# Half of the x transposes moved from TensorE to VectorE, and the first loads in another order

## The chip, the cores and the metric

The kernel runs on one core of a Trainium2 chip. A core has five engines that run at the same time, each with its own queue of instructions: TensorE (PE: matrix products, and transposes as products with an identity matrix; its weight loads are listed as PEld), VectorE (DVE), ScalarE (ACT), GpSimd (POOL) and SyncE (SP, which here only issues transfers). An engine works through its queue in the order in which the instructions stand there. PE's results go to PSUM, eight banks of 128 partitions x 512 numbers; everything else lies in SBUF, 128 partitions wide. Transfers between DRAM and SBUF run on 16 DMA engines; SP, ACT and POOL issue them.

The metric is the device time of one execution in microseconds (us), less is better. The kernel before takes 1168.65 us, the median of three runs (1167.21 to 1170.46).

## The reference

All numbers are float32. Four sequences of 512 tokens with 512 features each go through two layers (weight names without their prefix):

```python
# layer 0, V = 512, hidden size 4 V = 2048
q, k, v = x @ Wq, x @ Wk, x @ Wv
attn = softmax(einsum('btd,bTd->btT', q, k) * V ** -0.5)
attn_out = einsum('btT,bTd->btd', attn, v) @ Wp + bp
cms_out = gelu(attn_out @ cW1 + cb1) @ cW2 + cb2 + one_hot(target_codes)[:, None, :]
modifier = gelu(concat([attn_out, cms_out]) @ mW1 + mb1) @ mW2 + mb2
x = clip(x + cms_out + modifier, 0, 1)
# layer 1: an adapter chosen per sequence from three (stream)
h = gelu(x @ W_down[stream] + b_down[stream]) @ W_up[stream] + b_up[stream]
out = layernorm(x + h) * ln_w[stream] + ln_b[stream]
```

## The kernel before

**Products.** Every large product is split by a scheme with seven half-sized products in place of eight, and most of them twice. The price is sums of blocks, ahead of the products (operands) and behind them (results). The function `seven` (L622) runs the products in a given order; 1, 5 and 6 each open a PSUM bank, and 2, 7, 4 and 3 add to a bank that is there. Between them DVE makes sums on those banks: after 5 `c15 = ps + c1`, after 6 `y = x + c15`, after 7 `v = x + c15`, after 4 `x = x + c1`. Product 7 adds to the bank x and so waits until y has been made from it; product 4 waits in the same way until v has been made; product 3 adds to y. `pair_product` (L663) handles two sequences at once; one product in it is four matmuls of 128 x 512 (L668), some 3.43 us. `small_product` works on one 512 x 512 matrix (L734).

**The first stage.** Wq and Wk are turned on PE (L899) and folded into one matrix Wq Wk^T, likewise Wv and Wp into Wv Wp, so that scores are x (Wq Wk^T) x^T and the output is (softmax x) (Wv Wp). Sequences come in two pairs. For a pair the code makes x^T of both sequences (`first_operand`, `both_operands`), the product u with the folded Wq Wk^T (`pair_product` with `beside_u`, which makes the sums of u beside it), the two score products with softmax, softmax times x, and the product with the folded Wv Wp.

**How x is turned.** `begin_transposed` (L500) takes four PSUM banks and does 16 PE transposes of 128 x 128 (L505); its `end` copies each bank to SBUF on ACT and makes the block sums on DVE straight from PSUM. x1 and x2 are turned at the start. x3 and x4 are turned during the first pair's product with Wv Wp, after product 6 and after product 4 (`then`, L1011). That product and the next pair's first one then share the eight banks with the transposes.

**How Wv is turned.** `begin_turned` (L518) uses DVE's own transpose, which turns blocks of 32 x 32: `load_blocks` (L151) lays Wv in SBUF in such a way that turning the blocks alone gives Wv^T, with a fixed order of the features; Wp's rows are loaded in the same order. Four DVE transposes of 128 x 512 (L522) write four banks. They read every fourth element of a partition (`p (t c d) -> p d t c`). Transposes and sums are hung behind product 6 of the first pair's u product.

**Loads and places.** SP issues Wq in four quarters, x1, x2, Wv's four pieces, Wp. ACT issues Wk, later the stores of x^T (`xT_kept`) and of the attention output. POOL issues the first unit of cW1 and the rows of x3 and x4, then forms sums of weights for later stages (`expansion`), which it stores to DRAM; it also makes the block sums of x (`left_sums`) and of Wp (`right_sums`, L767). Large tiles are used several times: `slot[2]` and `slot[3]` hold Wv and Wp, `slot[4]` and `slot[5]` cW1's unit, `slot[6]` and `slot[7]` x3 and x4 by rows.

**Order.** A scheduler lays the instructions into each engine's queue; `tc.keep_in_program_order` pins single ones, and `steps` releases portions of POOL's expansion work behind a given instruction. A transfer issued by SP or ACT uses one of eight semaphores in turn, and waits for the transfer that last used it.

**Later.** The hidden layers (L1179, L1269, L1337, L1437 are their products) read weights through SP; `with_input` (L1717) reads `xT_kept` back and adds it to the result on POOL (L1719, L1722).

## Time and profile before

| what | us |
|---|---|
| median of three runs | 1168.65 |
| the profiled execution | 1168.84 |
| its span, first to last instruction | 1166.9 |
| PE busy | 1156.4 |
| DVE, POOL, ACT busy | 888.9, 589.2, 293.5 |
| first stage (attention, both pairs) | 0 to about 242 |
| first and second hidden layers, adapters | about 242 to the end |

The granted clock of PE is 0.999 of full speed. The profile's groups give the line of the code, engine, operation, and the tiles as out<-in with buffer numbers left out, followed by partitions x elements and the count; in the timeline start and length come first, and in brackets the idle time before the instruction and what ended it. A float32 matmul is recorded as two PE instructions, so one of 128 x 512 takes 0.857 us in two records. Busy times of single PE records overlap, since matmuls are pipelined; starts are the better measure. The chain of work that ended last gives start, length and work.

### The profile page before, as it was taken

The numbers are of one execution on the slowest core, as the hardware profiler recorded it, in microseconds if no ns is written. First come the engines' busy times: TensorE is split into PE (matmuls) and PEld (weight loads), VectorE is DVE, ScalarE is ACT, GpSimd is POOL, SyncE is SP. The second block draws the span as 40 slices with busy tenths as digits, with TensorE's granted clock in tenths as the row PEclk, the third lists the DMA queues.
The fourth block names the chain that finished last, engine by engine and source line by source line (L and its number), as shares of the span: only waits on it lengthen the run. The fifth ranks groups of instructions, "written<-read, shape, count | busy, mean of one in ns | idle before, by whom it ended". The sixth has DMA issues, their size and how long they took to land.

```text
span 1166.9 us, 13700 instructions
## 1 busy us (share of the span) xinstructions
PE 1156.4 (99%) x4973; PEld 925.0 (79%) x4973; DVE 888.9 (76%) x1219; ACT 293.5 (25%) x535; POOL 589.2 (50%) x652
## 2 busy tenths in 40 slices
PE   9999999999999999999999999999999999999997
PEld 7588558656468888888888887778888888888875
DVE  6855555467699967899699956689994588689956
ACT  4244316236520000012310037271000003230014
POOL 4889999988998057872200626972000001242101
PEclk9999999999999999999999999999999999999999
DMA  9762784997776588896847562146745455594701
GB/s 300 277 201 85 296 319 147 341 375 268 276 256 244 180 276 311 330 327 257 261 154 275 195 215 90 64 146 181 295 136 189 163 218 179 176 309 165 248 6 72
DMA packets 82450, 256.78 MB, mean 220 GB/s; under 512 B 7972, under 2 KB 41040, under 8 KB 67024
## 3 DMA queue, kind: packets, MB, share of 16 engines
q1 hardware_dynamic: 58032, 152.98, 36.8%
q0 software_dynamic: 21968, 93.37, 22.6%
q10 hardware_dynamic: 2384, 9.57, 2.0%
q8 instruction: 39, 0.64, 0.2%
q14 instruction: 27, 0.22, 0.1%
HBM read 186.69 MB, written 66.06 MB: 217 GB/s over the span
## 4 chain that ended last, share of the span: by engine, by line
PE 93%; DVE 4%; DMA 1%; issue 1%; DVEq 0%; SPq 0%
PE i L1437 29%; PE i L1337 24%; PE sum L734 10%; PE sum L1179 9%; PE sum L668 8%; PE c L1269 6%; PE down_ps L1543 2%; PE up_ps L1562 2%; DVE hidden L578 1%; PE tr_ps L505 1%; DMA wslot<-in_L_cond_mW 1%; DVE part L1041 1%; DVE slot L219 1%; PE up_ps L1557 1%; DMA wide<-in_L_cond_Wq 0%
## 5 line engine op out<-in xcount | busy, mean ns | idle before, releaser
L1337 PE MATMUL i<-slot,wslot 128*128 128x256 f32 x1184 | 261.5, 379 | 1.8 <-DVE part L1041 1.7
L1337 PEld LDWEIGHTS i<-slot,wslot 128*128 128x128 f32 x1184 | 224.7, 190 | 33.4 <-issue 1.8
L1437 PE MATMUL i<-slot,wslot 128*128 128x256 f32 x896 | 202.5, 379 | 0.0
L1437 PEld LDWEIGHTS i<-slot,wslot 128*128 128x128 f32 x896 | 170.2, 190 | 23.1
L1048 ACT COPY first<-i 128x256 f32<-128x256 f32 (+1 forms) x56 | 26.8, 479 | 518.7 <-PE i L1437 245.1
L1437 PE MATMUL i<-hidden,wslot 128*128 128x256 f32 x576 | 132.2, 379 | 0.0
L1437 PEld LDWEIGHTS i<-hidden,wslot 128*128 128x128 f32 x576 | 109.4, 190 | 15.7 <-issue 1.0
L1041 DVE TENSOR_TENSOR part<-i,part 128x512 f32<-128x512 f32 (+1 forms) x156 | 90.8, 591 | 36.8 <-PE i L1337 25.5
L1070 ACT ACTIVATE hidden<-hidden,bias 128x512 f32<-128x512 f32 x128 | 83.9, 716 | 79.1 <-DVE hidden L578 69.1
L1719 POOL DMA_DIRECT2D slot<-xT_kept x4 | 2.8, 692 | 152.9 <-PE i L1337 152.9
L1179 PE MATMUL sum<-mod,wslot 128*128 128x256 f32 x288 | 66.6, 379 | 0.0
L1179 PEld LDWEIGHTS sum<-mod,wslot 128*128 128x128 f32 x288 | 54.7, 190 | 7.4
L1041 DVE TENSOR_TENSOR part<-i,first 128x512 f32<-128x512 f32 (+1 forms) x62 | 36.3, 589 | 29.2 <-PE i L1337 17.5
L1722 POOL TENSOR_TENSOR cms<-cms,slot 128x512 f32<-128x512 f32 x16 | 22.4, 1419 | 69.9 <-PE i L1337 41.5
L219 DVE TENSOR_TENSOR slot<-hidden 128x1024 f32<-128x1024 f32 x46 | 57.6, 1252 | 0.0
L219 DVE TENSOR_TENSOR slot<-hidden,slot 128x1024 f32<-128x1024 f32 x46 | 56.7, 1233 | 0.3
L578 DVE TENSOR_TENSOR hidden<-part,hidden 128x2048 f32<-128x2048 f32 x20 | 55.0, 2748 | 0.5
L1269 PE MATMUL c<-slot,wslot 128*128 128x512 f32 x128 | 55.3, 592 | 0.0
L578 DVE TENSOR_TENSOR sum<-sum,wslot 128x512 f32<-128x512 f32 x48 | 33.2, 695 | 29.0 <-PE sum L734 19.2
L734 PE MATMUL sum<-hidden,wslot 128*128 128x256 f32 x232 | 53.2, 379 | 0.0
L1269 PEld LDWEIGHTS c<-slot,wslot 128*128 128x128 f32 x128 | 24.3, 190 | 30.6 <-issue 28.2
L734 PEld LDWEIGHTS sum<-hidden,wslot 128*128 128x128 f32 x232 | 43.8, 190 | 5.8
(339 smaller groups left out, 2123.9 us busy)
## 6 DMA issues: line engine op xcount, KB each, us to landing
wslot<-m_kept SPq DMA_DIRECT2D x48, 1024.0 KB, 6.4
wslot<-m_kept SPq DMA_DIRECT2D x36, 512.0 KB, 5.1
wslot<-c_kept SPq DMA_DIRECT2D x16, 1024.0 KB, 6.7
slot<-in_L_cond_mW POOLq DMA_DIRECT2D x24, 512.0 KB, 6.8
wslot<-in_L_cond_mW SPq DMA_DIRECT2D x24, 512.0 KB, 6.7
wslot<-in_L_cond_cW SPq DMA_DIRECT2D x40, 256.0 KB, 6.3
slot<-in_L_cond_cW POOLq DMA_DIRECT2D x16, 512.0 KB, 7.1
m_kept<-wide POOLq DMA_DIRECT2D x6, 1024.0 KB, 7.0
```

Source lines behind the costliest of these rows:

```text
L219: i = eng.tensor_tensor(out_, one, two, ALU.subtract)
L578: nc.vector.tensor_tensor(dst, a, b, ALU.add)
L668: nc.tensor.matmul(ps, lhsT=lhs[p][:, c, r * P : (r + 1) * P], rhs=rhs[p][:, c, :], start=(first_ and c == 0), stop=(c == 1), skip_group_c ...
L734: nc.tensor.matmul(v[:, j, :], lhsT=lhs[p][:, c, j * P : (j + 1) * P], rhs=rhs[p][:, c, :], start=(first_ and j == 0 and c == 0), stop=(c ...
L1041: nc.vector.tensor_tensor(dst, ps, other, ALU.add)
L1048: nc.scalar.copy(c1, p1)
L1070: nc.scalar.activation(block[:, t, :], block[:, t, :], AF.Gelu, bias=bias_c[:, 8 * half + t : 8 * half + t + 1],)
L1179: nc.tensor.matmul(halves_of(ps)[:, j, :], lhsT=a[g][:, at_[q], j * P : (j + 1) * P], rhs=rhs[q][:, 0, :], start=(first_ and j == 0), stop ...
L1269: nc.tensor.matmul(ps, lhsT=lhs(c, t), rhs=operands[p][:, c, :], start=(c == 0), stop=(c == 1),)
L1337: nc.tensor.matmul(out_ps[:, j, :], lhsT=a[j][q][:, c, :], rhs=now[q][:, c, :], start=(c == 0), stop=(c == 1),)
L1437: nc.tensor.matmul(ps[:, :256], lhsT=a[k // 2][q][:, k % 2, :], rhs=now[q][:, k, :], start=(k == 0), stop=(k == 3),)
L1543: nc.tensor.matmul(ps, lhsT=wd[:, c, n * P : (n + 1) * P], rhs=y[:, c, tokens], start=(c == 0), stop=(c == NV - 1),)
```

## The change

1. x3 and x4 are loaded as blocks by SP (`load_blocks`, four transfers each) into `slot[6]` and `slot[7]` and turned by DVE, as Wv is (`begin_x` chooses). Their rows, which `left_sums` and a later product need, are loaded by SP into the same places after the turning. x1 and x2 stay on PE, but all x^T now hold feature 4p+d in partition p, chunk d; so the PE transposes of x1 and x2 read their weights with a step of four elements, Wq and Wk are loaded with that order of rows, and `xT_kept` is written and read with it.
2. Wv's DVE transposes read 32 neighbouring elements (`p (t d c)`); Wp's rows are loaded to match, in four transfers.
3. SP issues, after x1 and x2, Wp, the first unit of cW1 (formerly POOL's), and Wv last. Wv lies in `slot[6]`, Wp in `slot[7]`, until x3 and x4 take these.
4. Wv's transposes are still hung behind product 6, its copies and sums now behind product 7. Wp's sums on POOL stand ahead of the first expansion steps, which are released behind the last of them.

```diff
-                out=w[:, 2 * r : 2 * r + 2, columns],
-                in_=src[rows, columns].rearrange("(c p) n -> p c n", p=P),
+                out=w[:, chunks, columns],
+                in_=src.rearrange("(p c) n -> p c n", c=4)[:, chunks, columns],
...
-    x_rows = [load_x(b, nc.sync, x_places[b]) for b in range(2)]
-
-    def load_blocks(src, dst, eng):
+    def load_blocks(src, dst, eng, order="p (t c d) -> p d t c"):
...
-        return dst.rearrange("p (t c d) -> p d t c", d=4, c=32)
-
-    wv = load_blocks(Wv, slot[2], nc.sync)
-    wp = slot[3].rearrange("p (c n) -> p c n", c=4)
-    nc.sync.dma_start(out=wp, in_=Wp.rearrange("(p c) n -> p c n", c=4))
+        return dst.rearrange(order, d=4, c=32)
+
+    x_rows = [load_x(b, nc.sync, x_places[b]) for b in range(2)]
+
+    def load_c1(u, eng):
...
+    wp = rows_of(slot[7])
+    for a in range(4):
+        nc.sync.dma_start(
+            out=wp[32 * a : 32 * a + 32],
+            in_=Wp[P * a : P * a + P].rearrange("(c p) n -> p c n", p=32),
+        )
+    load_c1(0, nc.sync)
+    wv = load_blocks(Wv, slot[6], nc.sync, "p (t d c) -> p d t c")
...
-        load_c1(0)
-
-        for b in range(2, B):
-            x_rows.append(load_x(b, nc.gpsimd, x_places[b]))
-        yield from expand_c1(0, lambda: load_c1(1))
+        yield from expand_c1(0, lambda: load_c1(1, nc.gpsimd))
...
-            nc.gpsimd.tensor_tensor(out_, one, two, ALU.subtract)
+            i = nc.gpsimd.tensor_tensor(out_, one, two, ALU.subtract)
+            if out_ is t1:
+                tc.keep_in_program_order(i)
+        behind.append(i)
...
-    xT_kept = [spill.tile([P, 4, 512], F32, name=f"xT_kept{b}") for b in range(B)]
+    xT_kept = [spill.tile([V, T], F32, name=f"xT_kept{b}") for b in range(B)]
...
+    def begin_x(b, dst, finish):
+        if b > 1:
+            return begin_turned(x_blocks[b - 2], dst, finish)
+        return begin_transposed(
+            lambda c: x_rows[b][:, c, :].rearrange("p (n d) -> p d n", d=4), dst, finish
+        )
...
         for k in range(2):
-            nc.scalar.dma_start(out=xT_kept[2 * pair + k], in_=xT[k])
+            nc.scalar.dma_start(
+                out=xT_kept[2 * pair + k].rearrange("(p c) n -> p c n", c=4), in_=xT[k]
+            )
+            if pair:
+                x_rows.append(load_x(2 + k, nc.sync, x_places[2 + k]))
...
+            rhs_wp = right_sums(wp, w_vp)
             steps(expanding, 2)
             s_v = sums_in(slot[2])
-            rhs_wp = right_sums(wp, w_vp)
-            then[6] = [lambda: begin_turned(wv, wv_t, left_from_psum(wv_t, s_v))()]
+            then[6] = [lambda: ends.append(begin_turned(wv, wv_t, left_from_psum(wv_t, s_v)))]
+            then[7] = [lambda: ends[1]()]
...
+            x_blocks = [load_blocks(x[b], flat(x_places[b]), nc.sync) for b in range(2, B)]
...
-            tc.keep_in_program_order(nc.gpsimd.dma_start(out=in_rows[3], in_=xT_kept[2 * pair + s]))
+            tc.keep_in_program_order(nc.gpsimd.dma_start(out=in_rows[3], in_=xT_kept[2 * pair + s].rearrange("(c p) n -> p c n", p=P)))
```

## The prediction

> **What bounds the kernel now.** I read the page's busy shares first, then the list of who made TensorE (PE) wait, then the chain that ended last, and only then the timeline around the places that the change touches.
>
> ```profile
> PE 1156.4 (99%) x4973; PEld 925.0 (79%) x4973; DVE 888.9 (76%) x1219; ACT 293.5 (25%) x535; POOL 589.2 (50%) x652
> ```
>
> ```profile
> PE i L1337 <- DVE part L1041: 1.7, 2, 1.4
> PE idle_ps L204 <- DVE zeros L201: 1.1, 1, 1.1
> PE sum L668 <- DVE sum L578: 0.9, 1, 0.9
> PE tr_ps L899 <- DMA wide<-in_L_cond_Wq: 0.4, 2, 0.2
> ```
>
> PE works through 1156.4 of 1166.9 us, and all its waits sum to 4.1 us. So only two things move the end: PE instructions that are removed or become longer, and waits of PE. The third wait line (0.9 us) lies where Wv is turned. In the chain (start, length, work) the reader is to see the transposes of the four x (L505, 16 each) as ordinary PE work in the row, and Wv's four VectorE (DVE) transposes (L522):
>
> ```profile
> 15.91 1.75 PE tr_ps L505 x16
> ...
> 23.03 1.90 PE tr_ps L505 x16
> 24.92 13.75 PE sum L668 x32
> 39.30 4.12 DVE tr_ps L522 x4
> 46.91 3.70 PE sum L668 x8
> ...
> 127.85 1.75 PE tr_ps L505 x16
> ...
> 134.00 3.44 PE sum L668 x8
> 137.44 1.64 PE tr_ps L505 x15
> 139.08 26.61 PE sum L668 x62
> ```
>
> The timeline at Wv: the transposes hold DVE's queue, eight small sums follow, and only then the two additions for which PE's product 4 waits.
>
> ```profile
> 39.30 4.11 DVE L522 STREAM_TRANSPOSE tr_ps<-slot 128x512 f32<-128x512 f32 x4
> ...
> 46.17 1.28 DVE L578 TENSOR_TENSOR sum<-sum,wslot 128x512 f32<-128x512 f32 x2
> ...
> 46.91 3.70 PE L668 MATMUL sum<-mod,cms 128*128 128x512 f32 x8 [0.88 <-DVE sum L578]
> ```
>
> **The change, part by part.** The sum is made against the profiled execution, 1168.84 us (span 1166.9 and 1.9 around it), 0.2 above the median of 1168.65.
>
> *PE loses the transposes of x3 and x4:* 16 at 127.85 (1.75 us), 15 at 137.44 (1.64) and a single one at 133.72 (0.11): 3.50 us, all in PE's row without a gap.
>
> *DVE gains eight transposes.* Price: the L522 row, 4.11 / 4 = 1.03 us each; they too read with a step of four elements. In the changed program's order they stand between DVE's additions. I follow that queue with the old starts. The sum for product 5 starts at 124.52 and the next can start 0.60 later. First transpose 125.12 to 126.15; addition for product 6 at 126.17, when PE delivers, as before; second transpose 126.77 to 127.80; addition at 127.88; third and fourth 128.48 to 130.54; eight small sums (2.74 in the old row at 130.34) to 133.25; then the addition that product 4 needs, 0.70 long, done at 133.95. PE now starts product 7 at 127.68 (where the transposes began), 3.43 for four matmuls, then three matmuls of product 3 (0.857 each): 133.68. So it waits 0.3 us. Below, the wait could be nothing; above, 1.0, the four transposes' 4.1 less the 3.1 of DVE idle time between 122.73 and 127.88 that they can fill. I take 0.3. For x4 the same walk has three transposes from 134.6 to 137.7, one addition, the fourth transpose to 139.4, and the first t1 that the next product 5 needs at 140.0; PE reaches it at 133.95 + 3.43 + 0.86 + 3.43 = 141.7, and its second chunk's t1 is done at 141.6 where it is wanted at 142.5. About a microsecond is left, so nothing is added. Gain of both: 3.50 - 0.3 = 3.2.
>
> *Wv's transposes read 32 neighbouring elements instead of every fourth.* No row shows a contiguous DVE transpose. Ends: 1.03 as now, or 0.60, the step from one 512-wide DVE instruction to the next (139.41 to 140.01). In the new order two, not eight, of the small sums stand ahead of product 4's addition, but PE also arrives earlier, since only half of product 3 stands ahead of product 4: 41.93 + 1.71 = 43.64 instead of 45.86. At 1.03 the addition ends at 39.30 + 4.11 + 0.68 + 0.70 = 44.8: PE waits 1.15, against 1.05 before and 0.18 of slow starts around it: gain 0.1. At 0.60 it ends at 43.1: no wait, gain 1.2. I take 0.60: source and destination are as in the 512-wide rows, and the step of four is what goes. Gain 1.2.
>
> *x1 and x2 stay on PE, but its weight loads now read every fourth element* (x[:, 4p+d]). All PE rows here read with step one, 1.75 / 16 = 0.109 us each. Low end: 0. High end, if a PE read is paced as the L522 row (1.03 us / 512 = 2.0 ns an element): 128 x 2.0 = 0.257 us, so 32 x 0.148 = 4.7 us, all of it on PE's row. I take 0, since the same instruction on the same engine is the nearest row, and keep 4.7 for the range; it is the largest doubt here.
>
> The Trainium skill (SBUF - State Buffer, section Door 1, its note on cachelines) speaks against this part: lines of 16 bytes, of which an access needs two hits to run at full rate. The 2.0 ns an element of the L522 row against 1.2 for a unit-step instruction fits it, though no run here shows it for PE. By that rule the 32 weight loads would about double, an estimate of 3.5 us, and the sum below would be 0.9 instead of 4.4.
>
> *Queues.* SP takes over four cW1 loads and Wp's, now four, ahead of Wv's four; later eight block loads and two row loads of x. POOL drops six issues (about 0.75 each) and its idle 9.7 us before L209 at 32.24 shrinks. No PE wait is on POOL, so this counts nothing. Hidden too: x3's and x4's blocks are issued when Wv's and Wp's buffers come free (from about 43 and 62) for use at 125 and 134; their rows again after their transposes, at 130.5 and 139.4, for POOL's sums at 157.8 and 191.2 (in_x rows took 9.5 to 17.9 us to land). POOL would queue behind them if late, and PE only at 188.6. SP has nothing else to issue until 205.5. Wq and Wk keep their pieces of 1 KB. The reads of xT_kept in pieces of 2 KB instead of 8 delay POOL's L1722 sums, which end at 579.5 in the first pair; DVE first uses them at 630. ACT's store of x2's transpose waits for a piece of Wp, issued about 20 us earlier: nothing.
>
> *Sum:* 3.2 + 1.2 - 0 = 4.4; 1168.84 - 4.4 = **1164.4 us**.
>
> **The rivals.**
> 1. *The strided weight loads cost.* For: the L522 row. Against: none of its time is PE's. At 1.7 times (1.03 / 0.60) 32 x 0.076 = 2.4 us, at the high end 4.7: 1166.8 to 1169.1, most likely about 1167.8. PE does the same work for x1 and x2 in more time than it saved on half of it.
> 2. *The contiguous transpose stays at 1.03.* 3.2 + 0.1: 1165.5.
> 3. *Slower: Wv lands late.* Its loads are now last, behind Wp and 2.1 MB of cW1, and each waits for an earlier load to land. DVE meets them at 39.3 in front of product 4's addition, and PE waits behind. From x's end (issued at 5.1, 9.5 to land: 14.6 us), Wp, cW1, Wv and the two stores of xT_kept are 6.3 MB; at the mean of 281 GB/s in the first 60 us that is 22.4 us: landed at 37.0. At 246 GB/s, what the DMA engines moved from 14 to 22 us while Wv and Wp came in, 40.2, already on the edge; at the 202 of the slowest 2 us in it, 45.8. It decides from about 39.9 on, and the time passes the old one when Wv lands after 44.3; a landing at 46 to 49 gives 1170.5 to 1173.5. Against: cW1, two x and the stores ran at 396 GB/s from 22 to 40 us; with that for cW1 and the stores (4.2 MB, 10.6 us) and 246 for Wp and Wv (2.1 MB, 8.5 us) Wv lands at 33.7. The same side holds a wait for x's rows or blocks that I have not seen.
>
> **How the numbers follow.** Chances: forecast 0.42 (own range 1163.3 to 1165.6), rival 1 0.31, rival 2 0.12, rival 3 0.15. About 0.3% (3.5 us) is what a measurement of this kernel can tell from no change; faster by more than that means below 1165.1. The forecast lies there for 0.37 of its 0.42, rival 2 for 0.04, rival 1 for 0.01: 0.42. Slower by over 0.3%, above 1172.2, is most of rival 3: 0.13. The rest, 0.45, is within. The range from 1163.2 to 1169.8 leaves out most of rival 3 and the edges of the others.
>
> **What would show it.** In the changed profile: L505's counterpart with two groups of 16 PE transposes fewer, and the two that stay (near 16 and 23 us) at 1.75 us each if step four is free, 3 to 4 us if rival 1 holds; Wv's DVE transposes at about 0.6 us and no PE wait near 44 us, or 1.03 and a wait of 1.1; the eight for x at 1.03 and a PE wait of 0.3 near 133. A DVE transpose released by a DMA near 40 us would show rival 3. After 140 us every PE start should be earlier by one constant; if it is not, a wait I have not named took the place.

## The result, and the profile after

| what | before | after |
|---|---|---|
| median of eight runs | 1168.77 us (1167.21 to 1170.46) | 1174.74 us (1170.64 to 1176.03) |
| the profiled execution | 1168.84 | 1174.30 |
| its span | 1166.9 | 1172.5 |

The ratio after to before is 1.0045 (95% interval 1.0029 to 1.0061): the changed kernel is slower by about half a per cent, where 1164.4 us, 0.4% faster, was forecast. Single executions lie up to 2 us from the median before and up to 4 us after; below, the profiled ones are compared with each other, and the medians decide whether a version is faster.

The page's first view, busy time, share of the span and instructions by engine, of after:

```profile
PE 1156.0 (99%) x4941; PEld 923.4 (79%) x4941; DVE 900.2 (77%) x1227; ACT 294.4 (25%) x535; POOL 596.7 (51%) x646
```

PE has 32 records fewer, as the change says, and is busy 0.4 us less, although the span is 5.6 us longer. So PE must have stood still somewhere; and since 3.5 us of transposes are gone, some of what remains must have become longer. Who made PE wait, in after (in total, times, longest; the first three lines):

```profile
PE i L1455 <- ACT first L1066: 7.3, 1, 7.3
PE idle_ps L223 <- DVE zeros L220: 1.1, 1, 1.1
PE tr_ps L915 <- DMA wide<-in_L_cond_Wq: 0.5, 2, 0.3
```

A single wait of 7.3 us is new, and it is in no part of the code that the change touches: L1455 (L1437 before) is the second product of the first hidden layer, some 200 us after the second loads of x3 and x4, the last of the edited transfers in the first stage. The waits that went are the one of 0.9 us at Wv and the one of 1.7 us at L1337, further behind. After's chain of work that ended last leads to the same place:

```profile
16.89 1.91 PE tr_ps L507 x16
...
24.17 2.12 PE tr_ps L507 x16
26.28 24.04 PE sum L670 x56
...
337.59 1.13 POOL slot L231
343.38 8.87 DMA m_kept<-first
352.82 72.83 PE i L1455 x328
```

Of before's chain, PE had nearly all. In after's, PE's unbroken row through Wv is there (26.28 to 50.32), but between 195 and 343 us the chain runs through POOL, which forms sums of weights for the next hidden layer and stores them; then through the store of the tile `first`, 8.87 us to land; then PE again. The one engine whose delay the prediction counted at nothing is in the chain for 12% of the span, 9 of the 12 between 195 and 343 us.

The place itself. PE's first work in this product, before and then after (start, length, engine, line, work, and in brackets the idle time and what ended it):

```profile
334.24 1.89 PE L1437 MATMUL i<-hidden,wslot 128*128 128x256 f32 x8
```

```profile
331.21 1.89 PE L1455 MATMUL i<-hidden,wslot 128*128 128x256 f32 x8
```

After's PE where it stops, and then its ACT:

```profile
343.59 1.89 PE L1455 MATMUL i<-hidden,wslot 128*128 128x256 f32 x8
352.82 4.41 PE L1455 MATMUL i<-slot,wslot 128*128 128x256 f32 x11 [7.34 <-ACT first L1066]
```

```profile
352.40 0.65 ACT L1066 COPY first<-i 128x256 f32<-128x256 f32 x2 [11.69 <-DMA m_kept<-first]
```

The same ACT row of before:

```profile
339.38 0.37 ACT L1048 COPY first<-i 128x256 f32<-128x256 f32 x1 [1.01 <-DMA m_kept<-first]
```

POOL's issue of the store that it waited for, and the next two loads that SP issues, before:

```profile
336.33 0.57 POOL L391 DMA_DIRECT2D m_kept<-first  x1
...
345.66 1.20 SPq L460 DMA_DIRECT2D wslot<-c_kept  x2
```

SP's of after (POOL's issue, at 343.38, is in the chain above):

```profile
342.92 1.20 SPq L462 DMA_DIRECT2D wslot<-c_kept  x2
```

The inner scheme of this product copies its product 1 from PSUM into the tile `first` on ACT. POOL's expansion uses the same tile for its last sum of the weight unit, and stores it; the copy can't overwrite it until that store has landed. Before, the store was issued at 336.33, landed about 3.0 us later, and the copy followed at 339.38. After, it was issued at 343.38, 7.05 us later, and took 8.87 us: SP had issued two loads of 1 MB at 342.92, half a microsecond ahead of it (before, SP's came 9.3 us behind it). The other versions agree: in the five profiles in which the copy waits for this store and SP's loads come 2.6 us or more behind it, the copy starts 3.05 to 3.7 us after the store's issue; in the three in which SP issues one within 1.5 us of it, after 6.7 to 9.7. PE goes on for as long as it has free PSUM banks. It had 64 matmul records (13.8 us) in eight banks: 331.21 to about 345. Then it stops, and from 352.82 it runs on at half rate for a while. After's busy time in stretches of 5 us:

```profile
core 0: us, PE busy (x) PEld busy (x) DVE busy (x) ACT busy (x) POOL busy (x), PEclk, DMA share, GB/s
345.00:350.00 5.00, 0.48 (x3) 0.07 (x1) 4.96 (x5) 0.00 (x0) 4.39 (x3) 0.96 0.96 346
350.00:355.00 5.00, 2.18 (x5) 1.82 (x6) 4.62 (x8) 0.65 (x2) 4.09 (x4) 0.50 0.66 264
355.00:360.00 5.00, 5.00 (x21) 4.23 (x21) 4.86 (x6) 0.00 (x0) 4.09 (x4) 0.86 0.02 0
```

The granted clock (PEclk) is 0.50 in the stretch in which PE starts again and 0.86 in the next. In single records: the first matmul takes 588 ns, the next seven 427, and those from the tenth on 216 (from start to start).

**The account.** PE reaches this product at 334.24 before and at 331.21 after: 3.03 us earlier, so most of the forecast gain (4.4) had been made by then. There it loses 9.67 us: 7.51 by standing still, 1.87 by eight records at half rate, 0.29 in small delays among the 64 records ahead of the stop. Behind it, gaps of 2.55 us that before has at 496 to 579 us are gone and 1.2 us of small new ones appear: 1.4 back. -3.03 + 9.67 - 1.4 = 5.24 of the 5.46 us between the two profiled executions; 0.2 us are not assigned.

DVE is late at the same place. Its last work ahead of the product, and its first addition in it, before and after:

```profile
321.32 3.56 DVE L1357 TENSOR_TENSOR wide<-hidden,hidden 128x2048 f32<-128x2048 f32 x1
...
337.51 2.27 DVE L1357 TENSOR_TENSOR wide<-hidden,hidden 128x2048 f32<-128x2048 f32 x1
...
346.57 0.75 DVE L1041 TENSOR_TENSOR cms<-i,first 128x256 f32<-128x256 f32 x2
```

```profile
318.29 7.13 DVE L1375 TENSOR_TENSOR wide<-hidden,hidden 128x2048 f32<-128x2048 f32 x1
...
341.28 4.30 DVE L1375 TENSOR_TENSOR wide<-hidden,hidden 128x2048 f32<-128x2048 f32 x1 [1.36 <-DMA m_kept<-wide]
...
352.80 0.76 DVE L1059 TENSOR_TENSOR cms<-i,first 128x256 f32<-128x256 f32 x2 [0.35 <-ACT first L1066]
```

DVE starts this work 3.03 us earlier, as PE does, but needs 34.2 us for what took 25.3 (to the end of its last work ahead of the product, 352.46 and 346.64): 3.6 more for the first subtraction (7.13 against 3.56), 1.8 for a smaller one behind it, at 329.94 (3.12 against 1.33), 1.4 of waiting for another of POOL's stores, 2.0 for a later subtraction (4.30 against 2.27). So even without the copy PE would have waited for DVE. Two suspects, then, that both lead back to a late POOL.

### The profile page after: what moved, and what is told of

It reads as the page before. It is cut to its first block, busy times and chain, and to the rows that moved or that the text cites. A ratio compares the mean times of both kernels' runs of the same rounds, so it can differ in the third digit from the quotient of the medians.

```text
span 1172.5 us, 13667 instructions
## 1 busy us (share of the span) xinstructions
PE 1156.0 (99%) x4941; PEld 923.4 (79%) x4941; DVE 900.2 (77%) x1227; ACT 294.4 (25%) x535; POOL 596.7 (51%) x646
## 4 chain that ended last, share of the span: by engine, by line
PE 78%; POOL 12%; DMA 6%; issue 2%; DVE 1%; ACT 0%; ACTq 0%; DVEq 0%; POOLq 0%
PE i L1455 28%; PE i L1355 28%; PE sum L736 8%; PE sum L670 5%; PE sum L1197 4%; DMA m_kept<-part 3%; PE down_ps L1561 2%; PE up_ps L1580 1%; POOL hidden L1227 1%; DMA wslot<-in_L_cond_mW 1%; POOL wslot L1189 1%; POOL part L228 1%; PE tr_ps L507 1%; POOL slot L366 1%; DMA m_kept<-first 1%
## 5 line engine op out<-in xcount | busy, mean ns | idle before, releaser
L1455 PE MATMUL i<-slot,wslot 128*128 128x256 f32 x896 | 204.5, 382 | 7.4 <-ACT first L1066 7.3
L1455 PEld LDWEIGHTS i<-slot,wslot 128*128 128x128 f32 x896 | 171.2, 191 | 31.8 <-ACT first L1066 7.7
L1455 PE MATMUL i<-hidden,wslot 128*128 128x256 f32 x576 | 132.2, 379 | 0.0
L1455 PEld LDWEIGHTS i<-hidden,wslot 128*128 128x128 f32 x576 | 109.4, 190 | 15.7 <-issue 1.0
L1740 POOL TENSOR_TENSOR cms<-cms,slot 128x512 f32<-128x512 f32 x16 | 26.9, 1709 | 70.7 <-PE i L1355 38.2
L238 DVE TENSOR_TENSOR slot<-hidden 128x1024 f32<-128x1024 f32 x46 | 61.7, 1341 | 0.0
L580 DVE TENSOR_TENSOR hidden<-part,hidden 128x2048 f32<-128x2048 f32 x20 | 49.1, 2453 | 0.5
```

The source lines that it names most:

```text
L238: i = eng.tensor_tensor(out_, one, two, ALU.subtract)
L580: nc.vector.tensor_tensor(dst, a, b, ALU.add)
L1455: nc.tensor.matmul(ps[:, :256], lhsT=a[k // 2][q][:, k % 2, :], rhs=now[q][:, k, :], start=(k == 0), stop=(k == 3),)
L1740: nc.gpsimd.tensor_tensor(cms[s][:, d, :], cms[s][:, d, :], in_rows[3][:, d, :], ALU.add)
```

## The experiments

### Which of the two holds PE: the copy behind the store, or DVE's row

The first three inner schemes of this product get another place for the copy, so that ACT needn't wait for POOL's store. In the changed kernel:

```diff
-        if len(z11.shape) == 3:
+        if in_place:
+            c1 = z11
+        elif len(z11.shape) == 3:
...
+                in_place=begun_layers[0] == 1 and i < 3,
```

> The changed kernel, but in the first c2 layer ScalarE copies the first product of the first three inner schemes into the block that these schemes fill (z11), not into `first`, so that this copy no longer waits for GpSimd's last store of `first`. Theory A (the loss is the one PE wait of 7.3 us near 345 us, with 1.9 us of half-rate matmuls behind it): both go, 1174.7 - 9.2 = 1165.5 us, between 1164.5 and 1167. Rival B (GpSimd is late as a whole, and the next of its buffers stops PE a little later): 1170 or more, with a new PE wait on a DMA or a GpSimd store after 352 us. Rival C (the loss lies in the moved transposes and loads themselves, and the wait only shows it): 1172 or more with no PE wait near 345 us.

Measured: 1172.29 us, ratio to before 1.0029 (1.0017 to 1.0041). Its PE waits:

```profile
PE i L1458 <- DVE cms L1061: 4.1, 1, 4.1
```

Most of the wait is still there, and it is DVE's now (its first addition at 351.69). The copy alone costs at most some 2.5 us by the medians, and the intervals of the two ratios overlap; the second theory, DVE's row, holds the rest. The same edit in the kernel before:

> The kernel before, with the same edit of the copy. Its copy waited 1.0 us for the store, but PE had 13.9 us of matmuls ahead of it and did not stop. Theory A: no change, 1168.7 within 1 us. Rival: if PE was held there unseen, 1 us less, 1167.6.

Measured: 1167.27 us, ratio 0.9993 (0.9983 to 1.0003): no difference. Before, the copy is early enough: PE's banks last to 348.2, the copy starts at 339.38, and there are 8 us to spare.

### Is a late POOL enough by itself

The kernel before, with idle work for POOL in the expansion of the unit in question: six subtractions of 2.35 us, repeated into the same tile.

```diff
         tt(s3, a11, a21, ALU.subtract)
+        if last is not None and is_first and u == 3:
+            for _ in range(6):
+                tt(s3, a11, a21, ALU.subtract)
```

> The kernel before, with one 128x1024 subtraction on GpSimd in its last expansion repeated six times (6 x 2.35 = 14.1 us). Nothing else is changed. Theory A: the store of `first` goes out at 350.4 instead of 336.3 and lands 3 to 9 us later, at 353.4 to 359.4; PE's 13.9 us of work ahead end at 348.2, so it stops for 5 to 11 us, and 1 to 2 us of slow matmuls follow: 1175 to 1182. Rival (GpSimd's lateness does not reach PE): 1168.7 within 1 us.

Measured: 1182.95 us, ratio 1.0126 (1.0111 to 1.0141). Its PE waits:

```profile
PE i L1440 <- ACT first L1051: 9.1, 1, 9.1
```

Nothing but POOL was touched, and the kernel before gets the very wait of after, with 12 records at half rate behind it; the store was issued at 347.2. Half of it, three subtractions (7 us, about POOL's delay in after):

> The kernel before, with the 128x1024 subtraction repeated three times: GpSimd 7.05 us late, as in the changed kernel, and nothing else of the change. Theory A with both chains: the store of `first` goes out at 343.4 us; the copy comes at 346.4 to 349, near the end of PE's 13.9 us of work at 348.2; VectorE meets GpSimd's later work and reaches the c2 layer's additions 4 to 6 us later, near 351 to 352: a PE stop of 3 to 4 us and 1.5 us of slow matmuls, 1172 to 1175. Rival (7 us of GpSimd are covered by the 8.4 us that the copy had in hand): 1168.7 within 1 us.

Measured: 1171.76 us, ratio 1.0033 (1.0020 to 1.0046). The profiled execution, the quickest of its kind at 1169.2, has the store at 340.07, and PE's wait is on DVE:

```profile
PE i L1440 <- DVE cms L1044: 1.5, 1, 1.5
```

The store is only 3.7 us later than in before, since POOL began this unit 2.6 us earlier in this execution (294.73 against 297.37). Another 7 us of POOL's time in one unit thus costs the old kernel about 4 us by the medians, in this profile by way of DVE. PE reaches the product 3 us sooner in after and so has 3 us less cover, which makes after's loss the larger.

### Which part of the change delays POOL

x3 and x4 go back to PE, with their rows loaded once (by SP, early). Everything else stays: the order of the first loads, Wv's transposes, the strided weight loads.

```diff
-        if b > 1:
-            return begin_turned(x_blocks[b - 2], dst, finish)
...
-                x_rows.append(load_x(2 + k, nc.sync, x_places[2 + k]))
...
-            x_blocks = [load_blocks(x[b], flat(x_places[b]), nc.sync) for b in range(2, B)]
+            x_rows += [load_x(b, nc.sync, x_places[b]) for b in range(2, B)]
```

> The changed kernel, but x3 and x4 are loaded once, as rows, where their blocks were loaded, and turned by PE with strided weight loads as x1 and x2 are; nothing of x is loaded at 130 and 139 us. Two theories on why GpSimd ends its expansions 7 us later. D (the second load of x3 and x4, 2.1 MB in a stretch where the DMA engines are full, delays GpSimd's stores by 5 us and more): GpSimd's store of `first` goes out near 337 us, PE does not stop, and the time is that of the kernel before less 1.2 for Wv plus 1.1 for the later start and 0.7 for 64 strided weight loads: 1169.3, between 1168 and 1170.5. E (loads and order before 64 us are the cause): the store goes out near 343 us as in the changed kernel, PE comes 3.2 us later and stops 4 us: 1174 to 1175.

Measured: 1169.28 us, ratio 1.0005 (0.9996 to 1.0014); no PE wait at the product, POOL's store at 337.00. So the loss comes with turning x3 and x4 on DVE, and the saving of 3.5 us of PE time with it. What is left of the change sums to about nothing: 1.2 us gained at Wv, 1.1 lost at the start of the first stage (below), and 64 transposes with strided weight loads at 0.011 each, 0.7.

What turning on DVE adds besides DVE's work is traffic: x3 and x4 are loaded twice. POOL's timeline of after shows where it falls behind. Two waits of POOL on its own stores, which before doesn't have:

```profile
155.85 0.72 POOL L228 TENSOR_TENSOR wide<-wide 128x256 f32<-128x256 f32 x1 [1.41 <-DMA c_kept<-wide]
...
166.64 0.73 POOL L228 TENSOR_TENSOR part<-first 128x256 f32<-128x256 f32 x1 [3.40 <-DMA c_kept<-part]
```

From the sum that begins at 146.46 to the one that begins at 175.95 POOL takes 29.5 us; before, 24.6 (145.87 to 170.48) for the same instructions. SP issues the second loads of x3 and x4, 2.1 MB, at 130.81 and 139.2. The stretches around them, before and after (the last three columns are the granted clock, the DMA engines' busy share and GB/s):

```profile
130.00:140.00 10.00, 10.00 (x37) 5.31 (x36) 5.94 (x13) 5.12 (x10) 10.00 (x9) 1.00 0.49 196
160.00:170.00 10.00, 10.00 (x35) 6.37 (x34) 7.00 (x17) 3.01 (x6) 9.98 (x14) 1.00 0.69 289
```

```profile
130.00:140.00 10.00, 9.92 (x24) 4.26 (x23) 10.00 (x18) 5.93 (x10) 9.98 (x9) 1.00 0.87 299
160.00:170.00 10.00, 10.00 (x42) 7.69 (x41) 6.30 (x15) 2.24 (x4) 6.56 (x10) 1.00 0.86 344
```

In between, at 140 to 160 us, the share is 0.84 and 1.01 before, 0.97 and 1.02 after: the loads enter a stretch in which the DMA engines were nearly full, POOL's stores come back later, and POOL, which has few tiles, waits for them (busy 6.56 of 10 us instead of 9.98). To test this, the second load is put back alone, with x3 and x4 still turned on PE; it now loads what is there already:

```diff
-            return begin_turned(x_blocks[b - 2], dst, finish)
...
-                x_rows.append(load_x(2 + k, nc.sync, x_places[2 + k]))
+                x_rows[2 + k] = load_x(2 + k, nc.sync, x_places[2 + k])
```

> The kernel with x3 and x4 turned by PE (e3_x34_on_PE), with one thing put back: after x3 and x4 have been turned, SyncE loads the rows of both a second time, where the changed kernel does. Theory D (this second load is what delays GpSimd): GpSimd needs 29.5 us instead of 24.6 from its subtraction into `first` near 147 us to the next into `part`, ends its expansions near 342 us instead of 337.0, VectorE and the copy come late to the c2 layer, and the time is 1172 to 1175. Rival (the second load is hidden; the eight transposes on VectorE or PE's earlier arrival make GpSimd late): 24.6 us for that stretch and 1169.3 within 1 us.

Measured: 1173.48 us, ratio 1.0047 (1.0029 to 1.0065): 4.2 us over the version without it by the medians. POOL's store is issued at 343.01 instead of 337.00, and PE waits 2.1 us on DVE, with seven records at half rate behind. But POOL lost its time elsewhere than I had said: not in the stretch from 147 (24.6 us, as before), but just ahead of it,

```profile
142.19 0.73 POOL L228 TENSOR_TENSOR part<-slot 128x256 f32<-128x256 f32 x1 [4.29 <-DMA c_kept<-part]
```

which is another store, caught by the same loads. And the reverse, the changed kernel without the second load:

```diff
-                x_rows.append(load_x(2 + k, nc.sync, x_places[2 + k]))
+                x_rows.append(x_places[2 + k])
```

> The changed kernel without the second load of x3 and x4: GpSimd's sums and PE's products of the second pair read the blocks as they lie, so the output of sequences 3 and 4 is not the reference's, while every instruction but the two loads stays. Theory D (the second load is what costs): GpSimd ends its expansions near 338 us instead of 343.4, PE does not stop in front of the c2 layer, and the 3.2 us that PE is ahead there are kept: 1165 to 1167. Theory F (VectorE's own queue in front of the c2 layer, full from 320 us on, eats PE's lead even with GpSimd in time; it was only 1.6 us ahead of PE in the kernel before): 1167.5 to 1169.5, with a PE wait on VectorE near 346 us.

Measured: 1166.52 us, ratio 0.9996 (0.9980 to 1.0012), 8.2 us below after by the medians; store at 339.35, PE waits 1.5 us on DVE. Its executions scatter widely, from 1164.1 to 1174.7; by the ratios, each to the kernel before beside it, the difference is 5.7 us. This version reads the blocks where the rows should lie, so it computes something else with the same instructions. Its store lies within the 335.6 to 339.6 us of the versions that leave the loads of x3 and x4 as they were before. Adding the load to a version that was well, and taking it from the one that is ill, move the time by 4.9 and 5.7 us by the ratios, 4.2 and 8.2 by the medians, both with POOL's store moving by 4 us or more. That the second load is the cause is shown.

The other suspect was the first load, the early blocks: SP issues them from 43 us on, and POOL, 9 us ahead of before when it ends the same sum at 47.6 us (before: 56.6), waits 8.46 us until 56.03 and 4.26 until 63.99 and has lost its lead at 88. ACT issues them later, behind the next stage's loads:

```diff
-            x_blocks = [load_blocks(x[b], flat(x_places[b]), nc.sync) for b in range(2, B)]
...
+                x_blocks = [load_blocks(x[b], flat(x_places[b]), nc.scalar) for b in range(2, B)]
```

> The changed kernel, but ScalarE issues the eight block loads of x3 and x4 between 70 and 105 us, where the DMA engines are a quarter busy, instead of SyncE from 43 to 64 us. The second load of the rows stays. Theory E (the early block loads take GpSimd the 6 us that it is ahead at 47 us, by its waits of 8.5 and 4.3 us): GpSimd is 4 us ahead or more at 88 us, so it ends near 338 us in spite of the second load; PE does not stop in front of the c2 layer or for a microsecond at most: 1165 to 1167. Rival (those waits have another cause): GpSimd is where it was at 88 us, and the time is 1173 to 1176.

Measured: 1174.39 us, ratio 1.0052 (1.0036 to 1.0068), as after. POOL's wait until 56.01 is 7.86 us, with the blocks or without them on the way, and it stands at 88.7 as in after. That theory falls: POOL's early lead ends with something else. Blocks and rows both later (the rows issued by ACT, at 134.2 and 146.1 instead of 130.8 and 139.2):

> As e6_blocks_later, and the second loads of x3's and x4's rows are ScalarE's too, x4's behind its two stores of attn. If the second load costs GpSimd 5 us because the DMA engines are full from 114 to 166 us: part of this comes back, GpSimd ends 2 to 4 us sooner than in e6_blocks_later, and the time is 1164.5 to 1166.5. Rival (only the amount counts, not when): as e6_blocks_later within 1 us.

Measured: 1171.55 us, ratio 1.0043 (1.0024 to 1.0063). POOL's store is still at 343.27; POOL now waits 5.76 us for a store of its own, until 169.06, so the second load only met another one. Its profile has two PE waits, 2.6 us on DVE at the product and 2.4 us at Wv, since Wv landed late in this execution: the third rival of the prediction, in one place.

### Why DVE is slow when POOL is late

In after, DVE's first large subtraction (two tiles of SBUF to a third, 128x2048) takes 7.13 us; unhindered it takes 2.28. POOL's timeline beside it:

```profile
318.55 0.74 POOL L231 TENSOR_TENSOR slot<-slot,slot 128x256 f32<-128x256 f32 x1
319.24 0.72 POOL L232 TENSOR_TENSOR slot<-slot 128x256 f32<-128x256 f32 x1
319.92 0.72 POOL L233 TENSOR_TENSOR slot<-slot,slot 128x256 f32<-128x256 f32 x1
320.60 2.33 POOL L380 TENSOR_TENSOR first<-slot,slot 128x1024 f32<-128x1024 f32 x1
322.89 0.57 POOL L383 DMA_DIRECT2D m_kept<-slot  x1
323.48 2.52 POOL L228 TENSOR_TENSOR part<-part 128x256 f32<-128x256 f32 x1
325.97 2.83 POOL L232 TENSOR_TENSOR part<-part 128x256 f32<-128x256 f32 x1
```

DVE's instruction starts at 318.29 and ends at 325.42. Up to 322.89 POOL runs sums one behind the other; then it issues a transfer, for 0.57 us. From that issue on, 323.14 (2.28 before the end), DVE would have had just the time that it needs. Now it is POOL whose next two small sums take 2.52 and 2.83 instead of 0.7: they wait for DVE in turn. The Trainium skill (SBUF — State Buffer, section Who interferes with whom) says that a DVE instruction with two SBUF inputs and a GpSimd instruction that reads SBUF shut each other out for the whole of an instruction. The rows agree that they do, and add that the one shut out needn't get in when the instruction ends: DVE waited through several. The same reckoning (its end less 2.28) for this instruction in all ten profiles in which it takes 3 us or more puts DVE's entry at an issue of a transfer by POOL in nine. The tenth is before itself: there DVE got in at about 322.6, between two of POOL's sums, with no transfer issued.

Two versions ask for it directly, by handing DVE the sums that POOL makes of the second pair's rows (`left_sums`). In the changed kernel, to free POOL of 10 us of work:

```diff
-        left_sums(x_rows[s0], s_x[0])
+        if not pair:
+            left_sums(x_rows[s0], s_x[0])
...
+            if pair:
+                left_sums(x_rows[s0 + k], s_x[k], pinned=True, eng=nc.vector)
```

> The changed kernel with the left sums of x3 and x4 (four 128x512 subtractions each, 5.1 us of GpSimd each) given to VectorE between the softmax steps of the second pair, at 0.6 to 0.7 us each. Both second loads stay. Theory A (GpSimd's end decides): it ends 8 to 10 us sooner, near 334 us, PE does not stop, and the time is 1164.5 to 1167, if VectorE's 2.7 us hold PE up for no more than 1 us near 180 and 196 us. Rival (the loss does not hang on GpSimd's end): 1172 or more.

Measured: 1168.84 us, ratio 1.0020 (1.0001 to 1.0039). POOL's store comes at 336.50 and no PE wait at the product is left; but this says little for the theory, since in this execution (1175.38 us, one of the longer ones) PE comes to the product 11 us later than in after (342.42). DVE's new sums, 0.69 us each when alone, took 3.15, 3.42 and 2.71 us beside POOL, and PE waited for them at 181 and 204 us:

```profile
PE sum L738 <- DVE sum L582: 6.4, 2, 4.2
```

What POOL gains is spent in another place. The same in the kernel before:

> The kernel before, with the same sums of x3 and x4 on VectorE. PE did not stop for GpSimd there, so theory A expects no gain: 1168.7 within 1 us, up to 1170 if VectorE's sums hold PE up. A gain of more than 1 us would say that the kernel before lost time to GpSimd too.

Measured: 1183.83 us, ratio 1.0131 (1.0110 to 1.0152). Its PE waits, and the DVE and POOL rows behind the longest of them:

```profile
PE sum L736 <- DVE sum L580: 13.9, 2, 11.3
```

```profile
204.97 12.31 DVE L212 TENSOR_TENSOR hidden<-hidden,slot 128x512 f32<-128x512 f32 x1
217.20 1.21 DVE L213 TENSOR_TENSOR hidden<-slot 128x512 f32<-128x512 f32 x1
```

```profile
205.27 2.37 POOL L376 TENSOR_TENSOR part<-slot,slot 128x1024 f32<-128x1024 f32 x1
...
216.25 0.57 POOL L379 DMA_DIRECT2D m_kept<-part  x1
```

A 0.69 us subtraction lasted 12.31 us: POOL ran nine sums without a break from 205.27 to 216.25, and DVE got in when POOL issued a transfer, and not between two of the nine. If a pause of POOL is what lets DVE in, small pauses should help: the changed kernel with a memset of one element a partition after each of POOL's sums in this unit (and with the copy elsewhere).

```diff
+    def with_gap(*args):
+        with tc.issue_after(last_gap[-1].ins) if last_gap else nullcontext():
+            i = nc.gpsimd.tensor_tensor(*args)
+        with tc.issue_after(i.ins):
+            last_gap.append(nc.gpsimd.memset(gap, 0.0))
+        return i
```

> The changed kernel with the copy elsewhere (as e1_copy_elsewhere), and between any two subtractions of GpSimd's last expansion a memset of one column, so that VectorE, which there adds pairs of SBUF tiles, can get in after each of them; the last expansion's work is in program order. Theory G (a VectorE instruction with both inputs in SBUF is held up until GpSimd's unbroken run of subtractions ends, as the 12.3 us of one 128x512 subtraction in e11_before_sums_on_DVE say): VectorE's 128x2048 subtraction near 318 us takes 3 to 5 us instead of 7.1, it reaches the c2 layer's additions 3 to 5 us sooner than the 351.7 of e1_copy_elsewhere, PE stops there for 2 us at most, and the time is 1167.5 to 1170.5. Rival (each takes turns anyway, or GpSimd loses as much by the breaks): 1171.5 or more, with VectorE's instruction at 6 us or more.

Measured: 1176.12 us, ratio 1.0070 (1.0056 to 1.0084). DVE's subtraction:

```profile
320.13 5.14 DVE L1391 TENSOR_TENSOR wide<-hidden,hidden 128x2048 f32<-128x2048 f32 x1
```

It stood through four memsets of 0.1 us and got in at the next issue of a transfer (323.05). As I put it, that theory falls: a pause of 0.1 us is not enough, or a memset is no pause. What exactly passes the lock on isn't settled. The total is worse for another reason: DVE waits 7.66 us later on, for POOL by the profile. The likely cause, not tested, is the order that the memsets need: POOL issues the store of `wide`, which DVE is to overwrite, at 342.55 instead of 337.00.

The last test takes POOL's sums out rather than apart: the inner sums of the unit, about 20 us of POOL's time, are left out in the changed kernel (what is stored in their place isn't the sums).

```diff
-                inner_sums(a, t[:, 1024:])
+                if not (last is not None and is_first and u == 3):
+                    inner_sums(a, t[:, 1024:])
```

> The changed kernel with the inner sums of GpSimd's last expansion left out (seven groups of four 128x256 subtractions, 20 us of GpSimd; what is stored for that unit of mW1 is not the sums, so the output is not the reference's). Both second loads and everything before 300 us stay. Theory A: GpSimd is done near 323 us, VectorE's sums run unhindered, PE does not stop in front of the c2 layer, and the whole gain of the forecast appears: 1163.5 to 1166. Rival (VectorE's queue or the start costs as much): 1167 or more with a PE wait on VectorE near 346 us.

Measured: 1165.70 us, ratio 0.9973 (0.9964 to 0.9982): faster than before. DVE's row at the product:

```profile
319.54 2.28 DVE L1378 TENSOR_TENSOR wide<-hidden,hidden 128x2048 f32<-128x2048 f32 x1
...
342.41 0.75 DVE L1062 TENSOR_TENSOR cms<-i,first 128x256 f32<-128x256 f32 x2
```

DVE is there 4 us sooner than in before, and no PE wait is left at the product. Would the kernel before have gained as much from less work on POOL?

> The kernel before with the same inner sums of GpSimd's last expansion left out as in e14_less_pool (so what is stored for that unit of mW1 is not the sums). If the kernel before lost nothing to GpSimd in front of the c2 layer, it stays at 1168.7 within 1 us, and the gain of e14_less_pool (3.5 us on the kernel before beside it) is the change's own. Rival: it gains 2 us or more as well, and the change's own gain is 1.5 us at most.

Measured: 1169.06 us, ratio 0.9999 (0.9990 to 1.0008): nothing. So with POOL out of the way the change is worth about 3 us (0.9973 against 0.9999; 3.4 by the medians) of the forecast 4.4.

### The smaller parts

Wv's part alone, in the kernel before (Wv's order and Wp's rows, copies behind product 7; loads and x as before):

```diff
-    wv = load_blocks(Wv, slot[2], nc.sync)
+    wv = load_blocks(Wv, slot[2], nc.sync, "p (t d c) -> p d t c")
...
-            then[6] = [lambda: begin_turned(wv, wv_t, left_from_psum(wv_t, s_v))()]
+            then[6] = [lambda: ends.append(begin_turned(wv, wv_t, left_from_psum(wv_t, s_v)))]
+            then[7] = [lambda: ends[1]()]
```

> The kernel before, with the Wv part alone: Wv's blocks read contiguously by VectorE (Wp loaded in four pieces with the rows that this needs), and Wv's sums one product later. Loads, their order and x stay. If the term of 1.2 us in the sum was right: VectorE's four transposes at 0.60 us, no PE wait near 45 us, 1167.5 us or 1.2 less than the kernel before beside it, since GpSimd and VectorE still reach the c2 layer in time (VectorE had 1.6 us in hand there). Rival (VectorE's place in front of the c2 layer takes the gain back): no change within 0.5 us, with a PE wait near 347 us.

Measured: 1172.44 us, ratio 1.0033 (1.0021 to 1.0046): slower, where I expected a gain. The four transposes take 2.49 us instead of 4.11 and the wait at 45 us is gone, as said. PE then arrives earlier at the product with Wp, whose sums POOL makes:

```profile
PE sum L738 <- POOL cms L776: 2.2, 2, 1.8
```

Those waits, at 51 to 55 us, give the gain back. The kernel before with less work on POOL has 1.5 us of the same wait. POOL was 2.2 us late there, since its first unit of weights came later in this execution (12.06 us idle before its first sum at 34.51, 9.72 before). In after these sums stand ahead of the expansion, which is the fourth point of the change, so the wait does not occur. In this execution PE is 0.6 us late from the first products on, which the edit doesn't touch, and 2.19 us late from 57 us on; that stays so to the hidden layer's product, where PE doesn't stop, and is about the whole difference of the two profiled executions (1170.87 against 1168.84). What brings the medians another 1 us apart, this profile can't say.

Wq's and Wk's new order of rows alone, in the kernel before:

```diff
-                in_=src[rows, columns].rearrange("(c p) n -> p c n", p=P),
+                in_=src.rearrange("(p c) n -> p c n", c=4)[:, chunks, columns],
```

> The kernel before, with Wq and Wk loaded as the changed kernel does (rows 4p + c on partition p; pieces of 1 KB in both). As x keeps its order, the products with Wq and Wk mix rows: the times are the kernel's, the output is not. Theory: this layout is why PE reaches x2's transposes at 23.5 to 24.1 us instead of 22.4 to 22.9 in the programs that have it: 1.1 us more, 1169.8, and gaps between the transposes of Wq and Wk. Rival (the order of the later loads does it): 1168.7, with x2's transposes at 22.9 at the latest.

Measured: 1168.93 us, ratio 1.0004 (0.9995 to 1.0013): no difference that the total can tell. But the start of x2's PE transposes is to be had from every profile, and that tells more. With the old layout of Wq and Wk, in seven profiles: 22.96 to 23.63, mean 23.30. With the new one, in eleven: 23.81 to 25.21, mean 24.36. The two groups do not overlap: x2's transposes start 1.1 us later when Wq and Wk are loaded in the new order of rows. In ten of the eleven, 0.17 of it is x1's strided weight loads just ahead. This version, the only one of the eleven without the rest of the change, is the latest (25.21); PE waits 1.54 us for a piece of Wk in it, and 0.54 for one of Wq.

A version that computes everything and beats both kernels was not found. The fastest, before with its copy elsewhere (1167.27), can't be told from before; the two that are faster than that leave work out.

## Why the prediction was wrong, step by step

*The PE transposes of x3 and x4* (3.50 us, less a wait of 0.3). Right: the groups are gone, and PE waits 0.24 + 0.11 us at 133, in after's timeline. 3.15 against the 3.2 forecast. The eight DVE transposes took 1.03 to 1.11 us each, 1.03 forecast.

*Wv's transposes* (1.2 us). Right: after's timeline has them at 0.62 each, and PE's next product without a wait.

```profile
40.97 2.50 DVE L524 STREAM_TRANSPOSE tr_ps<-slot 128x512 f32<-128x512 f32 x4 [0.21 <-DMA slot<-in_L_cond_Wv]
...
45.01 2.31 PE L670 MATMUL sum<-mod,cms 128*128 128x512 f32 x5
```

The bracket, 0.21 us of waiting for Wv's load, shows how near the third rival was: the landing, about 41, is 1.1 later than the point of 39.9 from which that rival was to decide; PE, which was 1.4 later too, didn't wait for it here. In other profiles with this order of loads, PE did wait there: 0.29 us (copy elsewhere), 0.76 (less POOL), 1.49 (gaps) and 2.38 (blocks and rows later), each time behind transposes that Wv's load released. So this rival holds now and then, and costs up to 2.4 us.

*Weight loads with a step of four elements* (0, with 4.7 as the upper end). Nearly right. PE's weight loads, before and after (the numbers behind the count are shortest, median and longest in ns, then the stretch in us):

```profile
L505 PEld LDWEIGHTS tr_ps<-ident,hidden x32: 138/140/143, 15.5 to 24.5; 128*128 128x128 f32 x32
```

```profile
L507 PEld LDWEIGHTS tr_ps<-ident,hidden x32: 196/209/218, 16.5 to 25.9; 128*128 128x128 f32 x32
```

The load itself takes half as long again (209 against 140 ns), but it runs beside the transpose ahead of it, and the spacing of the transposes goes from 109 to 120 ns: 32 x 11 = 0.35 us. The rule of the Trainium skill that the prediction weighed (SBUF — State Buffer, section Door 1), by which the estimate was 3.5 us, is nearer to what the load itself does than to what PE's row loses.

*Queues: Wq and Wk keep their pieces of 1 KB* (0). Wrong by about 1 us, the later start above (0.97 between before and after). The pieces keep their size and land later nevertheless; why, the runs don't show.

*Queues: "No PE wait is on POOL, so this counts nothing", and the rows of x3 and x4, "Hidden too".* This is the step that failed. It reads the list of PE's waits as if it held the bounds of every engine. What it holds is the waits that there are; how near another engine is to becoming one can't be seen in it. Two slacks had to be worked out, and both were in the trace of before: PE's eight banks at the product last to 348.2, while ACT's copy waits for POOL's store (there is a row that says so, with 1.01 us, ended by that store), a slack of 8.4 us; and DVE's first addition, at 346.57, had 1.6 us left. POOL also takes DVE's time wherever both read SBUF: the 3.56 us of DVE's first subtraction, in a list whose usual length is 2.27, was the sign of it. I followed the second loads to their users (POOL's sums at 157.8 and 191.2) and found them in time. I didn't follow them to those they displace on the DMA engines: POOL's stores, from 140 to 160 us, a stretch in which the DMA engines were busy 0.84 to 1.01 of the time already. At the same sums POOL is 0.6 us behind before's at 146 us and 5.5 at 176. From there the delay didn't just stay: it is 7.9 at 221, 12.5 at 266 and 6.9 at 304, as POOL meets waits for its own stores in both kernels, at other places and of other lengths; at the product it is 7.05. Without the second load it is 0.0 at 171 and 2.7 at 300. What makes it grow between 221 and 266, no run separates.

The sum, by its own terms: forecast -4.4; the part of it that reached the product was, by PE's starts, -3.17 - 1.22 + 0.97 + 0.39 = -3.03; then +9.67 at the product, of which 1.87 are PE's slow start after a stop, which the prediction did not have at all; -1.4 behind it.

*The rivals.* The first and the second did not come. The third had the right sign and the wrong place: Wv's landing was near its bound, and its last sentence, "a wait for x's rows or blocks that I have not seen", names the transfers that did it but not the one that waited; x's rows came in time, and what waited was everything behind POOL. The last test in the prediction is the one that tells: after 140 us every PE start was to be earlier by one constant. It was, by 3.03 us from 141 us up to the product's first start (334.24 against 331.21), and from 345 on it was not.

## What to carry to other kernels

An engine that is busy without a break and stands in nobody's list of waits is not free: for each of its results work out when the user would need it and how much is left, and where that is a few microseconds, count a delay of that engine as time. A transfer that is early enough for its own user can still push others back; look at the busy share of the DMA engines in the stretch where it moves, and at which short stores in it gate a chain. Where a product holds a whole set of PSUM banks behind one copy, the banks are the cover (13.8 us here), and it shrinks by what is gained ahead of it.

## What the runs showed of the hardware

- A DVE operation with two SBUF inputs was held by a whole run of POOL operations, not by one: 12.31 us instead of 0.69, over nine of them. It got in when POOL issued a transfer (0.57 us), and not at memsets of 0.1 us; so did another one in nine of the ten profiles in which it was held (3.3 to 7.1 us instead of 2.28), and once, in before, it got in between two POOL sums.
- After a stop, PE runs on at half rate for a while (427 ns from one matmul record to the next instead of 216): 8 records after a stop of 7.5 us, 6 to 12 after stops of 4.2 to 4.3, 12 after 9.3. Stops of 2.77, 1.93, 1.71 and 1.67 us had none behind them, but three of 2.25 to 2.7 (in the versions with the second load put back and with sums on DVE) had 7 or 8. In the traces the granted clock behind such a stop is at half for 3.41 us or a multiple of it. The Trainium skill (TensorE: Matmul & The Clock Gate, section Part 1: The HAM clock gate) has a window of idle time of about 3.4 us that halves the clock; the stops of over 4 us agree, and the three of 2.25 to 2.7 us are shorter than it. A wait of PE of 4 us or more thus costs some 1.3 to 3 us on top of itself (6 to 12 records at 0.211 more, and up to 0.4 at the first).
- POOL's store of 512 KB took 3.0 us (in before, the DMA engines 0.90 busy) and 8.87 us beside two 1 MB loads, the first issued 0.46 us ahead of it on another queue.
- A DVE transpose of 128x512 float32 takes 0.62 us when it reads neighbouring elements and 1.03 with a step of four. PE's weight load takes 209 ns instead of 140 with a step of four, of which 11 ns show in the row.
